# Layer 0 of a four-layer transformer kernel: order of the loads, place of the router's sums and of the mask's comparison

## The chip, the cores and the metric

The kernel runs on one core of one Trainium2 chip. The time is the device time of one execution in microseconds (us), as the median of three runs. Profiles come from one execution under the hardware profiler; times inside it count from the start of its span. TensorE (PE) does matrix products, VectorE (DVE) and ScalarE (ACT) work on rows of 128 partitions, GpSimd (POOL) sends the indirect DMAs here, and SyncE (SP) issues most of the plain DMAs, in its own order. PEld is TensorE's weight load.

## The reference, cut to what matters

Four layers, each of the form x = x + ffn(cond(x)), on x of shape (2, 1024, 256) in float32, so 2048 tokens. The change is in layer 0 and in one preparation for layer 1.

```python
def _L0_cond_ref(Efou, y, weight):
    ys = y * scale
    d = rsqrt(einsum('bi,io->bo', ys * ys, weight * weight) + EPS)
    return einsum('bsi,io->bso', Efou * ys[:, None, :], weight) * d[:, None, :]

def _L0_ffn_ref(x, gate_w, shared..., routed...):
    shared_out = _swiglu(x, shared_gate_w, shared_up_w, shared_down_w)   # width 512
    logits = x @ gate_w                                                  # 32 experts
    topk_ids, topk_val = argmax(logits), max(logits)
    xs = x * sigmoid(topk_val)
    # each token's row goes through the swiglu of its one expert (width 512)
    return shared_out + routed_out
```

Layer 1's attention takes a mask of (1024, 1024) bytes, `where(mask, scores, neg)`. The inputs have 1024 equal mask rows. The kernel compares them on the chip: where all rows are equal it uses a short form of layer 1, else a general one.

## The kernel before

x lies as `XT` (channels on partitions, two halves of 128 by 2048 tokens) and later as `Xt` (tokens on partitions). Layer 0, in `_layer0`, goes through these steps:

1. The conditioning weight `W` is loaded, squared (L425), and multiplied with the squared condition (`pd`, L429). Then eight products `ph` (L441) of 128x512 give `HT`, scaled by `dd` on ScalarE. `XT`'s first 1024 tokens are loaded by the kernel's entry function, the rest here (`_wload`, L84).
2. `_logits` gives 32 logits for each token; `_top` takes the maxima (L173) and their indices (L175).
3. `_route_static` counts, in one-hot rows `oh`, running sums `cum` and two products into `R` (L562, L564), which row of the DRAM buffer `xbuf` each token goes to: 96 rows for each of 32 experts, and 21 overflow tiles behind them. `xbuf` is filled with zeroes first by a DMA from `k.zero`, which is a piece of the same buffer `ACC` that holds the token rows `Hr` (row tile 15).
4. For 16 tiles of 128 tokens, `_token_major` (L350) turns `HT` into rows on TensorE, ScalarE scales them by the router's score, and GpSimd scatters them to `xbuf` (L281). The same is done for `XT` into `Xt` on VectorE (L461), without a scatter.
5. `shared(tb)` runs the shared expert for token block `tb` of 512 tokens: for each of 4 slices `f` of the width, products `spg` and `spu` (L1360), Silu (L1365), the product `sa` on VectorE (L1367), and four products into `spo` (L1370). Blocks 0 and 1 stand here, blocks 2 and 3 after the slots.
6. `_layer1_pre` loads layer 1's small weights, compares the mask's rows with row 0 (L667, L668, four pieces of 256 rows), sums the differences on TensorE (L672), and prepares layer 1's constants in small products.
7. 24 slots of 128 rows (`Split`): each loads its rows `xs` from `xbuf` (L297, only after all scatters), turns them (`ps_cm`, copied to `xsT`, L1523), and runs products `fpg`, `fpu` (L1659), the product `fa` on VectorE (L1694), turns `fpt`, copied to `faT` (L1670, L1671), and products `fpo` (L1677). Weights of the experts (three of 512 KB each) stream through a ring of 20 places of 512 KB (L400). Results go to `ybuf`.
8. The sum `rare` of "mask rows differ" and "overflow tiles used" decides by a branch whether overflow slots and the general layer 1 run. With these inputs neither runs.

The order of instructions on an engine comes from a scheduler that fills the engines by priority (program order) and by its own estimates of durations; semaphores are set from that order. `_behind(k, inst, ref)` orders one instruction after another for the scheduler without a wait; `_after` makes a wait. PSUM tiles with one `tag` share a number of buffers (`mm` 4, `t` 2, `o` 2). `hook` in `_shared` is called after each slice's products:

```python
        if hook:
            hook(f, mul, mm)
```

Of the kernel before, what the change touches and what calls it, by code (L numbers as in the profile page):

```python
# [8 lines left out]
F32 = mybir.dt.float32  # L9
# [255 lines left out]
class Rows:  # L265
# [30 lines left out]
    def load(self, dst, src):  # L296
        i = self.k.nc.sync.dma_start(dst, src)  # L297
        _after(self.k, i, self.new)
        self.read.append(i.ins.name)

# [45 lines left out]
def _token_major(k, psum, src, t):  # L346

    ps = psum.tile([P, 2, P], F32, name="ps_tm", tag="t", bufs=2)
    for c in range(2):
        k.nc.tensor.transpose(ps[:, c, :], src[:, c, t * P:(t + 1) * P], k.ident)  # L350
    return ps.rearrange("p c d -> p (c d)")
# [32 lines left out]
def _layer0(k):  # L384
# [11 lines left out]

    def weights(src):
        ws = [k.ring.take().rearrange("p (c f) -> p c f", f=f) for f in (F, F, D)]
        for w, n in zip(ws, ("L0_r1", "L0_r3", "L0_r2")):
            nc.sync.dma_start(w, A[n][src].rearrange("o (c p) f -> p (o c) f", p=P))  # L400
        return ws

    with ExitStack() as ctx:
# [4 lines left out]

        W, Wb0 = k.ring.take().rearrange("p (n c f) -> n p c f", n=2, c=2)
        W2, Wb1 = k.ring.take().rearrange("p (n c f) -> n p c f", n=2, c=2)  # L410
        _wload(nc, W, A["L0_cond_weight"])
        gw = rp.tile([P, 2, E], F32, name="l0_gw")
        _wload(nc, gw, A["L0_gate_w"])
        _wload(nc, XT[:, :, S:N], A["xT"][:, S:N])
# [4 lines left out]
        nc.vector.memset(k.Hr[:, :, D:], NONE)  # L419
        _zero_rows(k, ybuf[NS * T:(NS + NOV) * T, :])  # L420
# [28 lines left out]
        m8, ixf = _top(nc, rp, lg, E, "l0")  # L449
        score = rp.tile([P, NT], F32, name="l0_score")  # L450
        nc.scalar.activation(score, m8[:, :, 0], AF.Sigmoid)
        k.x.begin()
        rows, eid, nov, end = _route_static(k, rp, k.pre, psum, ixf, E, C, NOV, "l0")
        for t in range(NT):
            nc.scalar.activation(Ht[:, t, :], _token_major(k, psum, HT, t), AF.Copy,
                                 scale=score[:, t:t + 1])
            k.x.scatter(k.Hr[:, t, :], rows[:, t:t + 1])


        for t in range(NT):  # L460
            nc.vector.tensor_copy(Xt[:, t, :], _token_major(k, psum, XT, t))  # L461

        for tb in range(2):
            shared(tb)
        _layer1_pre(k, k.pre, psum)

        rare = k.pre.tile([1, 1], F32, name="l0_raref")
        nc.vector.tensor_tensor(rare, k.differf[0:1, :], end[0:1, E - 1:E], ALU.add)
        any_ = k.pre.tile([1, 1], I32, name="l0_rare")
        nc.vector.tensor_copy(any_, rare)  # L470
        _router_biases(k, psum)

        ws = {}
        slots = Slots(k, pool, psum)
        split = Split(k, pool, psum, slots, F)
        for i in range(NS):
            lo, cols = i * T, []
# [8 lines left out]
            split.slot(i, cols)  # L486
# [5 lines left out]
    k.yrows = (NS + NOV) * T  # L492
    free = k.ring.i, set(k.ring.held)

    def slots_over():
        k.ring.held = set(held)
# [47 lines left out]
    with cmp.Else():  # L544
        with tc_pool(k, "l0p", 2) as pool, tc_pool(k, "l0ps", 4, PSUM) as psum:
            one(rest())
# [3 lines left out]
def _route_static(k, pool, keep, psum, ixf, E, C, nov, name):  # L550
# [8 lines left out]
    for t in range(NT):  # L559
        nc.vector.tensor_add(cum[:, t + 1, :], cum[:, t, :], oh[:, t, :])  # L560
    R = psum.tile([P, NT, E], F32, name=name + "_R", tag="mm")
    nc.tensor.matmul(R.rearrange("p t e -> p (t e)"), k.before,  # L562
                     oh.rearrange("p t e -> p (t e)"), start=True, stop=False)
# [80 lines left out]

def _layer1_pre(k, pp, psum):
# [6 lines left out]
    with ExitStack() as ctx:  # L652
        pool = ctx.enter_context(tc_pool(k, "l1pr", 1))

        m0 = pool.tile([P, S], U8, name="l1_m0")
        nc.sync.dma_start(m0, A["mask"][0:1, :].to_broadcast([P, S]))

        k.mh = pp.tile([P, TB], U8, name="l1_mh")
        for g in range(4):
            q = slice(32 * g, 32 * g + 32)  # L660
            nc.gpsimd.tensor_copy(k.mh[q, :], m0[q, (g % 2) * TB:(g % 2 + 1) * TB])
        dif = pool.tile([P, 8], F32, name="l1_dif")
        for i in range(4):
            mm = pool.tile([P, 2, S], U8, name="l1_mm", bufs=2)
# [1706 lines left out]
```

## Time and profile before

| | us |
|---|---|
| median of 3 runs | 1553.33 (1551.42 to 1553.47) |
| profiled execution | 1554.72 |
| its span | 1553.0 |
| first product of TensorE | 9.81 |
| start of the logits' products | 28.2 |
| first turn of slot 0 | 107.03 |
| last product of the last slot, about | 269.9 |

The mean granted clock of TensorE over the span is 0.977 of full speed. HBM reads are 284.86 MB and writes 50.76 MB. A row of the timeline gives start, length, engine, source line, operation, result and operands, and in brackets how long the engine had been idle and what released it. A row of a table of stages gives busy time of each engine in a stretch of the span, the granted clock of TensorE (1.00 is full), and what the DMA engines moved. "SPq" is SP's queue of DMA issues.

### The profile page before, as it was taken

The page shows a single profiled execution, that of the slowest core. Times are in us where ns is not written, and L with a number is a line of the kernel's source. Part 1 is how long each engine was busy: PE and PEld are TensorE (multiplying, and loading weights), DVE is VectorE, ACT ScalarE, POOL GpSimd, SP SyncE. Part 2 cuts the span into 40 slices and gives each one's busy share as a digit, 9 for nine tenths or more (in the row PEclk, how much of TensorE's full clock was granted, in tenths as well). Part 3 has the DMA queues.
Part 4 walks back from the last instruction along what each step waited for, and adds up shares of the span by engine and source line. Part 5 has one row for each costly group of instructions (what it writes and reads, how often), then busy time and mean ns, then how long its engine had stood idle before and what let it go on. Part 6 is the DMA issues. An engine that isn't in the chain of part 4 may idle for free. (4 is left out here: it accounts for less than half of the span.)

```text
span 1553.0 us, 23694 instructions
## 1 busy us (share of the span) xinstructions
PE 1470.2 (95%) x8649; PEld 1021.0 (66%) x8652; DVE 478.2 (31%) x1596; ACT 303.9 (20%) x642; POOL 285.2 (18%) x317
## 2 busy tenths in 40 slices
PE   6989999999999999999999999999999989998897
PEld 2543333444555886555699999999985547864675
DVE  3732222324411444421111111111114414446432
ACT  2311212123111212211111111111111212126222
POOL 0400000300331441033001001010010253420342
PEclk9989999999999999999999999999999999999799
DMA  9859995923211684051053254155517437762470
GB/s 253 273 201 332 337 352 175 255 72 123 96 48 35 195 252 136 0 214 52 28 185 116 94 190 174 36 184 184 180 34 263 139 122 246 214 218 83 146 250 19
DMA packets 184239, 252.43 MB, mean 163 GB/s; under 512 B 17111, under 2 KB 137823, under 8 KB 184112
## 3 DMA queue, kind: packets, MB, share of 16 engines
q1 hardware_dynamic: 164448, 210.92, 42.2%
q0 software_dynamic: 14176, 36.63, 6.6%
q10 hardware_dynamic: 5488, 3.25, 0.7%
q8 instruction: 72, 1.18, 0.3%
q14 instruction: 55, 0.45, 0.1%
HBM read 284.86 MB, written 50.76 MB: 216 GB/s over the span
## 5 line engine op out<-in xcount | busy, mean ns | idle before, releaser
L1370 PE MATMUL spo<-ring,sa 128*128 128x256 f32 x768 | 192.5, 393 | 20.2 <-DVE sa L1367 15.1
L1370 PEld LDWEIGHTS spo<-ring,sa 128*128 128x128 f32 x768 | 140.7, 192 | 101.9 <-DVE sa L1367 71.5
L281 POOL DMA_INDIRECT tbuf<-ys,sdst x114 | 112.1, 984 | 509.4 <-ACT ys L1635 381.9
L1367 DVE TENSOR_TENSOR sa<-ssg,spu 128x512 f32<-128x512 f32 x96 | 65.8, 686 | 327.3 <-PE spu L1360 287.3
L1628 DVE TENSOR_TENSOR fa<-fsg,fpu 128x512 f32<-128x512 f32 x72 | 49.5, 687 | 316.0 <-PE fpu L1623 316.0
L1623 PE MATMUL fpu<-xsT,ring 128*128 128x128 f32 x1152 | 140.4, 275 | 0.0
L1623 PE MATMUL fpg<-xsT,ring 128*128 128x128 f32 x1152 | 140.3, 275 | 0.0
L1623 PEld LDWEIGHTS fpg<-xsT,ring 128*128 128x128 f32 x1152 | 137.1, 192 | 1.9
L1623 PEld LDWEIGHTS fpu<-xsT,ring 128*128 128x128 f32 x1152 | 134.4, 192 | 0.0
L1632 PE MATMUL fpo<-ring,fa 128*128 128x256 f32 x576 | 130.3, 379 | 0.0
L1365 ACT ACTIVATE ssg<-spg 128x512 f32<-128x512 f32 x96 | 57.3, 597 | 347.7 <-PE spg L1360 217.5
L1632 PEld LDWEIGHTS fpo<-ring,fa 128*128 128x128 f32 x576 | 106.7, 190 | 13.0
L1360 PE MATMUL spg<-HT,ring 128*128 128x512 f32 x192 | 102.1, 621 | 5.4 <-issue 2.8
L1360 PE MATMUL spg<-XT,ring 128*128 128x512 f32 x192 | 97.5, 599 | 0.1
L1360 PE MATMUL spu<-HT,ring 128*128 128x512 f32 x192 | 91.6, 596 | 0.0
L1360 PE MATMUL spu<-XT,ring 128*128 128x512 f32 x192 | 90.4, 592 | 0.0
L1599 PE MATMUL cph<-xsT,ring 128*128 128x128 f32 x624 | 83.9, 277 | 6.7 <-DMA ring<-in_L_r 3.7
L1599 PEld LDWEIGHTS cph<-xsT,ring 128*128 128x128 f32 x624 | 76.0, 192 | 10.4 <-DVE sn L1527 4.8
L1606 PE MATMUL cpo<-ring,ch 128*128 128x256 f32 x312 | 80.1, 380 | 0.8 <-ACT ch L1602 0.8
L1627 ACT ACTIVATE fsg<-fpg 128x512 f32<-128x512 f32 x72 | 43.0, 597 | 169.7 <-PE fpg L1623 169.7
L1360 PEld LDWEIGHTS spu<-XT,ring 128*128 128x128 f32 x192 | 36.6, 191 | 43.8 <-issue 43.6
L1360 PEld LDWEIGHTS spu<-HT,ring 128*128 128x128 f32 x192 | 36.6, 194 | 41.9 <-issue 41.7
(574 smaller groups left out, 1656.5 us busy)
## 6 DMA issues: line engine op xcount, KB each, us to landing
ring<-in_L_w SPq DMA_DIRECT2D x108, 1024.0 KB
ring<-in_L_r SPq DMA_DIRECT2D x96, 512.0 KB
ring<-in_L_r SPq DMA_DIRECT2D x156, 256.0 KB
xs<-xbuf SPq DMA_DIRECT2D x138, 129.0 KB
ring<-in_L_W SPq DMA_DIRECT2D x32, 512.0 KB
yt<-tbuf SPq DMA_DIRECT2D x48, 256.0 KB
xbuf<-ACC SPq DMA_DIRECT2D x1, 6063.0 KB
ring<-in_L_s SPq DMA_DIRECT2D x6, 512.0 KB
```

Of the source, the lines that this page charges most:

```text
L281: i = k.nc.gpsimd.indirect_dma_start(out=self.ap, out_offset=bass.IndirectOffsetOnAxis(ap=idx, axis=0), in_=rows, in_offset=None, **end)
L1360: mm = nc.tensor.matmul(ps, W[:, c, f * P:(f + 1) * P], X[:, c, cols], start=c == 0, stop=c == 1)
L1365: k.silu = nc.scalar.activation(sg, pg, AF.Silu)
L1367: mul = nc.vector.tensor_mul(a, sg, pu)
L1370: mm = nc.tensor.matmul(po[g // 2][:, g % 2, :], a[:, g * P:(g + 1) * P], W2[:, f, :], start=f == 0 and g % 2 == 0, stop=f == nf - 1, skip ...
L1599: made = [nc.tensor.matmul(ph[:, f, :], R1[:, c, f * P:(f + 1) * P], xT[:, c, :], start=c == 0, stop=c == 1) for f in range(2) for c in ra ...
L1606: made = [nc.tensor.matmul(po, h[:, f, :], R2[:, f, :], start=f == 0, stop=f == 1) for f in range(2)]
L1623: made = [nc.tensor.matmul(ps[:, j, :], W[:, c, (f0 + j) * P:(f0 + j + 1) * P], xT[:, c, :], start=c == 0, stop=c == 1) for ps, W in ((pg, ...
L1627: nc.scalar.activation(sg, pg, AF.Silu)
L1628: nc.vector.tensor_mul(a[:, f0:f0 + 4, :], sg, pu)
L1632: made = [nc.tensor.matmul(po, a[:, f, :], W2[:, f, :], start=f == 0, stop=f == 4 * nh - 1) for f in range(4 * nh)]
```

## The change

- **Loads.** The conditioning weight is issued before `XT`; `XT` comes in four blocks of 512 tokens, then `gate_w`, then the shared weights. Four products of a tile of ones stand at the start of TensorE's work (`warm0`).
- **Clearing.** The filler column of `Hr` is set for tiles 0 to 14 only; tile 15 has it from `k.zero`. The 21 overflow tiles of `ybuf` are cleared in `slots_over`, in the branch for overflow.
- **Router.** Indices, `_route_static`, the turns of `HT` and the scatters move into the hook of shared block 0: all of the routing and tiles 0 to 7 at `f = 0`, tiles 8 to 15 at `f = 1`, `XT`'s turns for tiles 0 to 7 at `f = 2, 3`, and for tiles 8 to 15 in block 1. `_behind` ties index instructions to `mul` and TensorE's to `mm` of that slice.
- **Weights of experts 0 to 4** are issued before the slots' row loads, which are ordered behind the last of these 15 loads.
- **Mask.** The comparison leaves `_layer1_pre` for `_mask_rows`, a generator that is advanced once before each odd slot up to 17; it works in eight pieces of 128 rows. `rare` is formed after the slots' loop.

```diff
+        warm = psum.tile([P, 4, P], F32, name="warm0", tag="mm")
+        for _ in range(4):
+            nc.tensor.matmul(warm, k.ones, _bc(k.ones, 1, [P, 4, P]), start=True, stop=True)
...
         _wload(nc, W, A["L0_cond_weight"])
         gw = rp.tile([P, 2, E], F32, name="l0_gw")
+        for tb in range(NB):
+            _wload(nc, XT[:, :, tb * TB:(tb + 1) * TB], A["xT"][:, tb * TB:(tb + 1) * TB])
         _wload(nc, gw, A["L0_gate_w"])
-        _wload(nc, XT[:, :, S:N], A["xT"][:, S:N])
...
-        nc.vector.memset(k.Hr[:, :, D:], NONE)
-        _zero_rows(k, ybuf[NS * T:(NS + NOV) * T, :])
+        nc.vector.memset(k.Hr[:, 0:NT - 1, D:], NONE)
...
-        k.x.begin()
-        rows, eid, nov, end = _route_static(k, rp, k.pre, psum, ixf, E, C, NOV, "l0")
-        for t in range(NT):
-            nc.scalar.activation(Ht[:, t, :], _token_major(k, psum, HT, t), AF.Copy,
-                                 scale=score[:, t:t + 1])
-            k.x.scatter(k.Hr[:, t, :], rows[:, t:t + 1])
-        for t in range(NT):
-            nc.vector.tensor_copy(Xt[:, t, :], _token_major(k, psum, XT, t))
-        for tb in range(2):
-            shared(tb)
+        def stream(t, mm):
+            nc.vector.tensor_copy(Xt[:, t, :], _token_major(k, psum, XT, t, mm))
+
+        def lead(f, mul, mm):
+            if f == 0:
+                ix = rp.tile([P, NT, 8], U32, name="l0_ix", tag="ix")
+                for t in range(NT):
+                    _behind(k, nc.vector.max_index(ix[:, t, :], m8[:, t, :], lg[:, t, :]), mul)
+                ixf = rp.tile([P, NT, 8], F32, name="l0_ixf", tag="ixf")
+                nc.vector.tensor_copy(ixf, ix)
+                k.x.begin()
+                got[:] = _route_static(k, rp, k.pre, psum, ixf, E, C, NOV, "l0", mm)
+            if f < 2:
+                for t in range(8 * f, 8 * f + 8):
+                    nc.scalar.activation(Ht[:, t, :], _token_major(k, psum, HT, t, mm), AF.Copy,
+                                         scale=score[:, t:t + 1])
+                    k.x.scatter(k.Hr[:, t, :], got[0][:, t:t + 1])
+            else:
+                for t in range(4 * f - 8, 4 * f - 4):
+                    stream(t, mm)
+
+        got = []
+        shared(0, lead)
+        rows, eid, nov, end = got
+        shared(1, lambda f, mul, mm: [stream(t, mm) for t in range(8 + 2 * f, 10 + 2 * f)] if f < 4 else None)
         _layer1_pre(k, k.pre, psum)
...
-        ws = {}
-        slots = Slots(k, pool, psum)
+        ws = {e: weights(slice(e, e + 1)) for e in range(5)}
+        slots = Slots(k, pool, psum, ref=sent[-1])
         split = Split(k, pool, psum, slots, F)
+        muls = []
+        mask = _mask_rows(k, k.pre, pool, psum, muls)
         for i in range(NS):
+            if i < 18 and i % 2 == 1:
+                next(mask)
...
-            split.slot(i, cols)
+            muls.append(split.slot(i, cols))
...
     def slots_over():
+        k.yrows = (NS + NOV) * T
+        nc.vector.memset(k.zero[:, 0:D], 0.0)
+        _zero_rows(k, ybuf[NS * T:(NS + NOV) * T, :])
...
-def _route_static(k, pool, keep, psum, ixf, E, C, nov, name):
+def _route_static(k, pool, keep, psum, ixf, E, C, nov, name, ref):
...
+    i = nc.tensor.matmul(R.rearrange("p t e -> p (t e)"), k.before,
+                         oh.rearrange("p t e -> p (t e)"), start=True, stop=False)
+    _behind(k, i, ref)
...
+def _mask_rows(k, pp, pool, psum, muls):
+    nc, A = k.nc, k.A
+    m0 = pool.tile([P, S], U8, name="l1_m0", bufs=1)
+    nc.sync.dma_start(m0, A["mask"][0:1, :].to_broadcast([P, S]))
...
+    for i in range(8):
+        mm = pool.tile([P, S], U8, name="l1_mm", bufs=2)
+        nc.sync.dma_start(mm, A["mask"][i * P:(i + 1) * P])
+        yield
+        ne = pool.tile([P, S], U8, name="l1_ne", bufs=1)
+        _behind(k, nc.vector.tensor_tensor(ne, mm, m0, ALU.not_equal), muls[-1])
+        nc.vector.tensor_reduce(dif[:, i:i + 1], ne, AX.X, ALU.add)
+    d1 = pool.tile([P, 1], F32, name="l1_d1", bufs=1)
+    nc.vector.tensor_reduce(d1, dif, AX.X, ALU.add)
+    pd = psum.tile([P, 1], F32, name="l1_pd", tag="t", bufs=2)
+    nc.tensor.matmul(pd, k.ones, d1, start=True, stop=True)
...
+            load = self.k.x.load(self.xs[i], self.k.xbuf[i * P:(i + 1) * P, :])
+            if self.ref is not None:
+                _behind(self.k, load, self.ref)
...
-    _wload(nc, k.XT[:, :, 0:S], A["xT"][:, 0:S])
```

## The prediction

> **What bounds the kernel now.** I read the page's totals first, then a table of stages over the first 114 us, then the timeline of single waits, because the change touches nothing behind layer 0's 24 expert slots. The page says TensorE is busy 95% of the span, so only time in which it idles, or runs at a lowered clock, can be won.
>
> ```profile
> span 1553.0 us, 23694 instructions
> PE 1470.2 (95%) x8649; PEld 1021.0 (66%) x8652; DVE 478.2 (31%) x1596; ACT 303.9 (20%) x642; POOL 285.2 (18%) x317
> ```
>
> The chain that ended last gives nothing for the first 140 us, so the stages have to speak (columns: window, length, busy time and instructions of PE, PEld, DVE, ACT, POOL, granted clock, DMA share, GB/s):
>
> ```profile
> 0.00:10.00 10.00, 0.19 (x1) 0.19 (x2) 1.64 (x11) 1.28 (x1) 2.04 (x15) 1.00 0.64 212
> 9.80:28.20 18.40, 18.39 (x40) 8.79 (x40) 2.85 (x18) 5.01 (x8) 0.00 (x0) 1.00 1.11 287
> 28.20:48.00 19.80, 12.05 (x48) 6.01 (x48) 12.84 (x80) 6.34 (x13) 0.00 (x0) 0.74 1.10 288
> 48.00:82.00 34.00, 34.00 (x134) 20.42 (x132) 26.81 (x41) 10.66 (x18) 22.00 (x20) 1.00 0.68 231
> 82.00:107.03 25.03, 19.61 (x102) 12.99 (x101) 9.44 (x19) 4.08 (x8) 0.00 (x0) 0.84 0.73 251
> ```
>
> TensorE idles 9.8 us at the start, 7.7 us in 28.2 to 48 (routing) and 5.4 us in 82 to 107, and the clock falls to 0.74 and 0.84 there. In the timeline (start, length, engine, line, operation, in brackets the idle time before and its releaser) one sees by what:
>
> ```profile
> 9.81 1.87 PE L429 MATMUL pd<-l_ys,ring 128*128 128x2 f32 x8 [9.81 <-DVE ring L425]
> ...
> 42.95 0.09 DVE L419 MEMSET ACC<- 128x32 f32 x1 [2.29 <-DMA xbuf<-ACC]
> ...
> 43.15 1.13 PE L564 MATMUL l_R<-l_cum,ones 128*128 128x512 f32 x2 [2.00 <-DVE l_cum L560]
> ...
> 79.67 0.34 SPq L297 DMA_DIRECT2D xs<-xbuf  x1
> ...
> 83.56 2.29 DVE L667 TENSOR_TENSOR l_ne<-l_mm,l_m 128x2048 uint8<-128x2048 uint8 x1 [4.45 <-DMA l_mm<-in_mask]
> ...
> 86.50 3.78 PE L1370 MATMUL spo<-ring,sa 128*128 128x256 f32 x8 [4.03 <-DVE sa L1367]
> ```
>
> VectorE waits for the zeroing of xbuf at L419, and R behind it. SP's queue stands from 63 us until the scatters are done (79.67). Behind that stands the last mask load; VectorE waits for it, and shared block 1's product `sa` behind VectorE.
>
> From 107 us on the slots run without holes. A slot takes 6.18 us, or 6.97 us where two row tiles are turned first (121.15 to 127.33 to 134.30), and TensorE hardly waits for a weight.
>
> **Start.** Before, TensorE's first product waits for the weight, queued behind 1 MB of XT. It then runs cold: fp32 instructions of 512 columns come every 0.86 us until 17.2 us, then every 0.43. The change puts the weight (0.25 MB) ahead of XT and splits XT. The 2 KB `cT` load, issued at 0.83, was used at 4.44; so I put the weight at 5 to 6 us and XT's first quarter at 7 to 8 (estimates from that and the 1.3 MB landed by 9.06). The four added products of ones are 8 instructions x 0.86 = 6.9 us, from 1.2 (`ones` is set at 0.92) to 8.1. So they, not the loads, set the start: pd 8.1 to 9.05, then 32 instructions x 0.43 = 13.8, end 22.9 against 28.2: **-5.3**.
>
> Here the Trainium skill ("TensorE: Matmul & The Clock Gate", Part 1) gives a warm-up of about 3.4 us of sustained activity. By it the last four added instructions would take 0.43 each and the stage end 1.7 us earlier (-7.0). The trace needed 7.4 us here and 5.7 us after the hole at 86.5. I take the trace.
>
> Against splitting speaks the Trainium skill's "DMA: Bandwidth & Descriptors", Bandwidth: transfers of at least 1 MiB for 75% of peak; XT goes from two of 1 MB to four of 0.5 MB. Its 6.15 us for 1 MB (78%), had every half to be paid alone, would put XT's fourth quarter at some 15 to 18 us (estimate); TensorE wants it at 9.05 + 10.3 = 19.4, so the sum stays. The slots' own loads are 0.5 MB and move 350 GB/s, so I keep 10 to 12 us.
>
> **Logits to slot 0.** Before, 28.2 to 107.03 = 78.8 us. The work in it at full clock: spg and spu 64 x 0.43 = 27.5; spo 64 x 0.215 = 13.8; ps_tm 64 x 0.108 = 6.9; logits, their turn, R and cnt 4.0; layer 1's preparation 5.1; the mask's sum 0.3. Together 57.6, so 21.2 are lost: 13.2 idle, 8 clock and gaps.
>
> The change puts max_index and all of the routing behind the first `sa` product, with shared block 0 beside it, and ties the 32 turns of rows to its steps. The scheduler orders TensorE by its own estimates, which I can't see. Before, R's halves stood 2.4 and 2.0 us waiting. I take 3 us of such stalls (0 where shared products stand between, 10 where both halves are placed as badly as before and the clock falls too).
>
> The hole at 82.5 (4.0) and its cold stretch to 92.2 (half of 5.7, 2.9) go with the mask's comparison. So does the wait at L419, since the memset leaves row 15 alone. Layer 1's preparation stays serial: 1.5 idle, and 3 for clock and gaps. Thus 57.3 + 3 + 1.5 + 3 = 64.8, slot 0 at 22.9 + 64.8 = 87.7 against 107.0; this part gives **-14.0**.
>
> Can rows and weights be there? Logits end like before 3.4 us ahead of `lg`: 26.3, maxima 28.6, Sigmoid and Silu tables (1.28 each) and `sa` about 31.5. The old chain from index to rows took 33.84 to 53.02, less 2.3 for the wait: 16.9, and 2 for three `sa` between: rows at 50.4. Sixteen scatters took 53.9 to 78.0; four lasted 2.2 to 2.4 us, mostly under a mask comparison, instead of 0.96, so without it about 19 to 20: 70. xs is issued at about 72 and landed near 75.5, 12 us before slot 0. The xbuf zeroing landed at 42.95 with 2.7 MB of ybuf zeroes behind it; without them no later, and before 50. That removal therefore gives **0**; without this cover the scatters, then slot 0, would move one for one.
>
> The 15 loads of experts 0 to 4 now pass ahead of xs on SP: about 15 x 0.55 = 8 us of issue and 7.9 MB, 23 us at 350 GB/s, behind the zeroing; done by about 65, while xs waits until 72 anyhow: **0**. On SP the mask's nine loads leave the front and stand among the slots' weights. Each needs a buffer that VectorE freed two pieces before, so I price that at 0; if one waits, all weights behind it wait.
>
> **Slots.** Eight comparisons and eight reductions of 128x1024 bytes come to VectorE, half of the 2.28 us of the old 128x2048 rows: 1.14 each, 2.28 a slot. The gap that they fall into, from this timeline (`faT` of the same stretch starts at 129.88):
>
> ```profile
> 120.67 0.76 DVE L1523 COPY xsT<-ps_cm 128x256 f32<-128x256 f32 x2 [1.44 <-PE ps_cm L359]
> 125.67 0.69 DVE L1694 TENSOR_TENSOR fa<-fsg,fpu 128x512 f32<-128x512 f32 x1 [1.54 <-PE fpu L1659]
> 131.84 0.69 DVE L1694 TENSOR_TENSOR fa<-fsg,fpu 128x512 f32<-128x512 f32 x1 [1.54 <-PE fpu L1659]
> 133.82 0.75 DVE L1523 COPY xsT<-ps_cm 128x256 f32<-128x256 f32 x2 [1.30 <-PE ps_cm L359]
> ```
>
> After an even slot's `fa` VectorE is free for 3.5 us, after an odd slot's only 1.3 us before `xsT`, which TensorE awaits. The pieces are tied to even `fa`: they fit, price 0. On the other parity each would hold `xsT` by 1.0, 8 in all. I take **+1**, near the fitting end, because up to slot 16 the pairs stand before even slots. The mask's sum (0.3 on TensorE) and the branch's flag lie well before the last slot: 0, or up to 1.5 if the flag is ordered last. The added `ref`s only order; the ybuf clearing sits in a branch not taken here.
>
> **Sum.** -5.3 - 14.0 + 1 = -18.3. The profiled execution took 1554.7 us (span 1553.0): 1536.4. The median of the runs is 1.4 lower: **1535**.
>
> **Rivals.** (1) Routing only half hidden: both halves of R stall TensorE for some 4 us each, with cold clock after, as the old order did. That takes 8 to 10 off: about 1544. For it: the old trace shows TensorE standing there though shared products were ready. Against: the order is now tied to the shared block. (2) The scatters set slot 0. They must be 12 us later than reckoned, rows at 62; if at 66, slot 0 is 4 us later, and the time 1539; far worse only with the zeroing held up by weights, at rows near 72: 1545. (3) Slower: the slots starve. After slot 0 about 81 weight loads (42.5 MB), 2.7 of xs, 3.1 of ybuf and 1.2 of mask must pass in the 148 us up to slot 23's first product: 335 GB/s, where 323 over the stretch and 350 in its middle were seen, at TensorE's demand. If mask loads stop SP's queue so that the mean falls to 49.5/167 = 296 GB/s the gain is gone; at 280 the slots take 29 us more, and the result is about 1564. Against: the five experts held ahead are 25 us of cover. (4) It does nothing: the scheduler, moved by the new orders, builds the old holes elsewhere: 1553.
>
> **Chances.** Forecast 0.60 (its own range 1529 to 1540), (1) 0.15, (2) 0.08, (3) 0.12, (4) 0.05. A measurement tells 0.2%, 3 us, from no change. Faster 0.60 + 0.15 + 0.08 = 0.83, less a sliver of bad cases of (1) and (2), 0.82; same 0.05; slower 0.13. The range goes from the forecast's low end with the skill's clock and no stall, 1528, to 1550, beyond which lie (3), (4) and that sliver.
>
> **What would show it.** Right: pd near 8 us and instructions 0.43 apart soon after; no idle on R beyond 3 us; no hole at a `sa` in shared block 1; ps_cm of slot 0 near 88; slots still 6.2 and 7.0 us; the comparisons directly behind even `fa`. Wrong: PE waiting for `l_cum` or `l_oh`, for xs at slot 0, or for ring loads within the slots; `xsT` starting later behind a comparison.

## The result and the profile after

The changed kernel took 1559.33 us (median of 20 runs, 1553.04 to 1566.73), the kernel before 1553.80 in the 20 runs measured beside it. The ratio is 1.0037, with a 95% interval of 1.0024 to 1.0051: slower by 0.4%, where 1535 and "faster" had been forecast. In two other groups of runs, told of below, the same kernel came out 0.2% faster than the kernel before, and 0.5% slower.

The profiled execution took 1560.12 us, its span 1558.4. First the totals of the page of the changed kernel:

```profile
span 1558.4 us, 23706 instructions
PE 1473.9 (95%) x8660; PEld 1020.1 (65%) x8660; DVE 479.7 (31%) x1604; ACT 305.2 (20%) x643; POOL 281.2 (18%) x317
```

The span grew by 5.4 us: TensorE's busy time by 3.7, in which the 5.87 us of the added products of ones are counted, and its idle time by 1.7. So the idle time that was to go did not go. The table of stages of the changed kernel (window, length, busy time and instructions of PE, PEld, DVE, ACT, POOL, granted clock, DMA share, GB/s) says where; its windows are the start, `ph`, routing, two stretches of the shared blocks, and the slots:

```profile
0.00:7.72 7.72, 5.87 (x8) 2.23 (x9) 1.49 (x11) 1.28 (x1) 2.04 (x15) 1.00 0.47 123
7.72:22.54 14.82, 14.82 (x40) 6.89 (x40) 2.69 (x18) 5.01 (x8) 0.00 (x0) 1.00 1.10 317
22.54:47.40 24.86, 21.61 (x87) 11.17 (x86) 15.15 (x82) 11.08 (x17) 0.00 (x0) 1.00 1.11 232
47.40:74.14 26.74, 13.84 (x54) 8.67 (x53) 7.17 (x20) 6.17 (x12) 15.52 (x16) 0.80 1.06 378
74.14:105.22 31.08, 28.62 (x140) 17.51 (x140) 9.22 (x23) 5.29 (x10) 2.42 (x4) 0.94 0.22 67
105.22:278.70 173.48, 160.49 (x1432) 61.86 (x1427) 59.22 (x109) 33.48 (x73) 0.00 (x0) 0.97 0.81 278
```

The logits start at 22.54 instead of 28.2. Routing had 12.05 us of TensorE's work in 19.8 us before, and now has 21.61 in 24.86. But from 47.4 to 74.1 TensorE works for only 13.84 of 26.74 us, at a clock of 0.80. Slot 0 starts at 105.22, 1.8 us earlier than before and not 19. The slots take 173.5 us; the same stretch before took 165.57, from 107.03 to 272.6. The rest of the kernel is as long as before.

The timeline of the changed kernel (start, length, engine, line, operation, in brackets the idle time before and its releaser) shows the start and what stands in that stretch:

```profile
1.14 5.87 PE L416 MATMUL warm<-ones 128*128 128x512 f32 x8 [1.14 <-DVE ones L92]
...
6.97 0.69 DVE L436 TENSOR_TENSOR ring<-ring 128x512 f32<-128x512 f32 x1 [2.38 <-DMA ring<-in_L_cond_weight]
...
7.72 1.05 PE L440 MATMUL pd<-l_ys,ring 128*128 128x2 f32 x8 [0.71 <-DVE ring L436]
...
14.76 20.41 SPq L84 DMA_DIRECT2D l_wq<-in_L_Wq  x1
...
40.26 1.89 SPq L84 DMA_DIRECT2D l_sim<-in_L_sim  x1
42.20 2.28 SPq L759 DMA_DIRECT2D l_gts<-in_L_gates  x1
...
49.70 0.19 DVE L762 TENSOR_TENSOR l_sq<-l_sim 128x32 f32<-128x32 f32 x1 [6.31 <-DMA l_sim<-in_L_sim]
49.89 0.21 ACT L760 ACTIVATE l_gts<-l_gts 128x16 f32<-128x16 f32 x1 [7.79 <-DMA l_gts<-in_L_gates]
...
52.44 1.11 PE L351 MATMUL ps_tm<-ident,HT 128*128 128x128 f32 x4 [5.01 <-ACT ACC L481]
...
66.66 0.69 DVE L398 TENSOR_TENSOR Xt<-spo,Xt 128x512 f32<-128x512 f32 x1 [3.75 <-PE spg L1404]
71.56 0.69 DVE L398 TENSOR_TENSOR Xt<-spo,Xt 128x512 f32<-128x512 f32 x1 [4.21 <-remote]
...
73.66 0.42 DVE L467 COPY Xt<-ps_tm 128x256 f32<-128x256 f32 x1 [1.41 <-issue]
74.14 0.69 PE L351 MATMUL ps_tm<-ident,XT 128*128 128x128 f32 x2 [7.88 <-issue]
...
105.22 1.12 PE L362 MATMUL ps_cm<-ident,xs 128*128 128x128 f32 x4
```

There are two holes. **The first** (47.4 to 52.4): VectorE stands 6.3 us in the middle of the routing's chain for `l_sim`, ScalarE 7.8 us for `l_gts`, two loads of a few KB for layer 1. SP issued them at 40 and 42 us, because its queue had stood at `l_wq` from 14.76 to 35.2, behind the 6 MB zeroing of `xbuf`. **The second** (66.3 to 74.1): TensorE's row names no cause, but it starts when VectorE's copy of `ps_tm` at 73.66 has freed a place in PSUM (in e11 below the row names VectorE). VectorE's two sums come 3.8 and 4.2 us after the instruction before them. TensorE's last product of the `spo` that they read had ended at 64.95.

The kernel before had the same late loads, and they cost nothing there. From its timeline:

```profile
13.31 20.46 SPq L343 DMA_DIRECT2D ybuf<-ACC  x1
33.82 10.07 SPq L84 DMA_DIRECT2D l_wq<-in_L_Wq  x1
...
51.57 0.37 SPq L84 DMA_DIRECT2D l_sim<-in_L_sim  x1
```

SP's queue stood 30 us in all behind the two clearings, and `l_sim` went out at 51.57 us; but `l_sq` stood far behind in VectorE's order: it ran at 88.56 us, and did not wait.

In the slots there are three places. The waits of SP's queue in the changed kernel (us in all, times, longest):

```profile
SPq L696 <- DVE l_ne L699: 17.4, 6, 5.6
```

Six mask loads stood 17.4 us for the comparison that frees their buffer, with row loads behind them. The timeline of the changed kernel's TensorE, with idle time only:

```profile
208.05 0.41 PE L362 MATMUL ps_cm<-ident,xs 128*128 128x128 f32 x2 [1.64 <-DMA xs<-xbuf]
222.24 0.38 PE L704 MATMUL l_pd<-l_d,ones 128*128 128x1 f32 x2 [1.58 <-DVE l_d L702]
223.46 1.45 PE L1705 MATMUL fpg<-ring,xsT 128*32 128x512 f32 x8 [0.55 <-DVE l_rare L518]
```

TensorE waits for rows, at slot 17 for the mask's reduction, and one product later for the flag.

### The profile page after: what moved, and what is told of

Read it like the earlier page. It is cut to its first block, busy times and chain, and to the rows that moved or that the text cites. A ratio compares the mean times of both kernels' runs of the same rounds, so it can differ in the third digit from the quotient of the medians.

```text
span 1558.4 us, 23706 instructions
## 1 busy us (share of the span) xinstructions
PE 1473.9 (95%) x8660; PEld 1020.1 (65%) x8660; DVE 479.7 (31%) x1604; ACT 305.2 (20%) x643; POOL 281.2 (18%) x317
## 5 line engine op out<-in xcount | busy, mean ns | idle before, releaser
L1409 ACT ACTIVATE ssg<-spg 128x512 f32<-128x512 f32 x96 | 57.3, 597 | 347.5 <-PE spg L1404 250.5
```

Source lines behind the costliest of these rows:

```text
L1409: k.silu = nc.scalar.activation(sg, pg, AF.Silu)
```

## Experiments

Each group of runs was made together, with the kernel before measured in the same group; only ratios within a group are compared closely. "Slot 0" is the start of its first turn, "slots" the time from the first `fpg` of slot 0 to that of slot 23, both from one profiled execution of each kernel; before: 107.03 and 152.4, changed: 105.22 and 159.2. The kernel before has a profile of the first measurement only, so where a slot 0 or a stretch of slots is set against it, two groups are compared.

| Run | Group, before (us) | median (us) | ratio to before, 95% | slot 0 | slots |
|---|---|---|---|---|---|
| e1 small loads first | A, 1545.29 | 1536.91 | 0.9949 (0.9935 to 0.9963) | 89.46 | 160.1 |
| e2 four mask buffers | A | 1535.93 | 0.9940 (0.9924 to 0.9957) | 97.01 | 157.5 |
| e3 lazy weights | A | 1545.20 | 0.9996 (0.9981 to 1.0011) | 97.22 | 159.5 |
| e4 before + start | A | 1534.82 | 0.9932 (0.9912 to 0.9952) | 99.17 | 151.3 |
| e5 changed again | B, 1548.69 | 1546.33 | 0.9983 (0.9969 to 0.9996) | 97.55 | 159.4 |
| e6 before + mask | B | 1550.63 | 1.0013 (0.9998 to 1.0029) | 103.33 | 161.1 |
| e7 sum late | B | 1541.77 | 0.9954 (0.9938 to 0.9970) | 97.29 | 159.5 |
| e8 repaired | B | 1528.79 | 0.9865 (0.9838 to 0.9892) | 88.97 | 151.0 |
| e9 mask loads by GpSimd | C, 1553.81 | 1561.39 | 1.0045 (1.0030 to 1.0060) | 110.56 | 154.5 |
| e10 repaired, sum early | C | 1551.24 | 0.9982 (0.9965 to 1.0000) | 98.22 | 155.4 |
| e11 changed again | C | 1560.32 | 1.0052 (1.0035 to 1.0070) | 104.73 | 158.3 |
| e12 repaired + ybuf clear | C | 1545.76 | 0.9948 (0.9929 to 0.9966) | 98.64 | 151.9 |
| e13 repaired again | D, 1543.54 | 1530.37 | 0.9909 (0.9877 to 0.9941) | 88.84 | 151.4 |
| e14 repaired, lazy | D | 1528.29 | 0.9884 (0.9841 to 0.9927) | 90.67 | 152.1 |
| e15 no scatters | D | 1563.30 (one run) | | 92.21 | 152.1 |
| e16 memsets ahead | D | 1527.14 (one run) | | 89.09 | 152.2 |
| e17 loads last | E, 1543.17 | 1528.52 | 0.9906 (0.9890 to 0.9923) | 92.23 | 152.0 |
| e18 no scatters | E | 1551.60 (one run) | | 89.18 | 150.6 |

### The first hole: two small loads (e1)

```diff
+        k.sim = k.pre.tile([P, 2, 16], F32, name="l1_sim")
+        _wload(nc, k.sim, A["L1_sim"])
+        k.gts = k.pre.tile([P, 16], F32, name="l1_gts")
+        nc.sync.dma_start(k.gts, A["L1_gates"].to_broadcast([P, 16]))
         k.x = Rows(k, xbuf, [_zero_rows(k, xbuf)])
...
-        _wload(nc, sim, A["L1_sim"])
-        nc.sync.dma_start(k.gts, A["L1_gates"].to_broadcast([P, E]))
```

(The last two lines are in `_layer1_pre`; the added ones stand on L428.)

> The changed kernel, with only the two small loads l_sim and l_gts issued ahead of xbuf's zeroing. Theory 'small loads': the hole of 47.4 to 52.4 us on TensorE is VectorE and ScalarE standing for these two loads (6.31 and 7.79 us). Then rows come at about 46 us instead of 52, the hole goes with its cold stretch, slot 0 starts about 7 us earlier (near 98) and the time is about 1552. Rival 'order': the hole comes from the order of the turns and the routing's chain itself; then TensorE still stands some 4 us before the turn of HT, slot 0 stays near 105, and the time near 1559. The second hole (66.3 to 74.1) shows here too unless it was a single event of the profiled execution.

Timeline of e1, the same instructions:

```profile
14.69 0.34 SPq L428 DMA_DIRECT2D l_gts<-in_L_gates  x1
15.15 0.62 SPq L344 DMA_DIRECT2D xbuf<-ACC  x1
15.82 20.07 SPq L84 DMA_DIRECT2D l_wq<-in_L_Wq  x1
17.86 0.19 DVE L762 TENSOR_TENSOR l_sq<-l_sim 128x32 f32<-128x32 f32 x1 [7.37 <-DMA l_sim<-in_L_sim]
19.42 0.22 ACT L760 ACTIVATE l_gts<-l_gts 128x16 f32<-128x16 f32 x1
```

The queue still stands 20 us behind the zeroing; the two loads are now ahead of it, and `l_sq` and `l_gts` are done at 18 and 20 us, in time that nobody needs. The first hole is gone, TensorE works without a gap from 37 to 79 us, and slot 0 starts at 89.46. In e2 and e3 of the same group, the changed kernel with other mask buffers and with later expert loads, which have the first hole and not the second, it starts at 97.01 and 97.22, up to 7.8 us later. From 47.4 to 74.14 TensorE idles 5.8 us in e3, at a clock of 0.87, and not at all in e1, at 1.00. The theory of the small loads holds, and the rival "order" falls. By the medians e1 is 8.3 us faster than e3. (The expectation's 98 still counted with the second hole, which this group does not show.) The slots are no better than in the changed kernel.

### The second hole (e3, e5, e11, and e13 to e18)

```diff
-        ws = {e: weights(slice(e, e + 1)) for e in range(5)}
-        slots = Slots(k, pool, psum, ref=sent[-1])
+        ws = {}
+        slots = Slots(k, pool, psum)
```

> The changed kernel, without the early issue of the 15 expert loads: they are issued slot by slot as in the kernel before. TensorE, VectorE and ScalarE keep their orders. Theory 'crowding': the hole of 66.3 to 74.1 us comes from the DMA engines being full with the 15 loads (378 to 393 GB/s from 50 to 74 us), which makes VectorE's instructions late. Then the hole is gone, slot 0 starts 8 to 10 us earlier (near 96), and the time is about 1550, or 1555 if the first slots wait for weights. Rival 'scatters': the hole comes from GpSimd's scatters at the same time; then it stays, slot 0 near 105, time near 1559. Rival 'once': the hole is absent here and in the other runs as well.

e3 has no second hole, but e1 and e2 of the same group, with all 15 loads, have none either. So the group could not decide, and e5 ran the changed kernel unaltered:

> The changed kernel itself, unaltered, on the chip of the other experiments. With the four-buffer mask its first 97 us had the same orders and no hole at 66 to 74 us. Theory 'single event': the hole belongs to the one profiled execution or to its chip; then slot 0 starts near 97 here, the slots take some 8 us more than before, and the ratio to the kernel before is about 0.996 (97 + 8 against 107). Rival 'the change makes it': the hole of 7 to 8 us comes again, slot 0 near 105, ratio 1.002 to 1.005, and a second buffer pair for the mask would have to be what removed it.

Table of stages of e5, the stretch that held both holes and the next one:

```profile
47.40:74.14 26.74, 20.32 (x78) 12.70 (x78) 9.71 (x26) 6.83 (x14) 14.93 (x16) 0.87 1.07 380
74.14:97.55 23.41, 20.94 (x117) 13.29 (x115) 6.61 (x17) 4.64 (x9) 3.05 (x5) 0.96 0.34 110
```

Only the first hole is in it, and slot 0 starts at 97.55; the kernel is 0.17% faster than before. It would have been easy to take the second hole for one bad execution. But e11, the same kernel in group C, has it again:

> The changed kernel once more, unaltered. If the hole of 66 to 74 us is a single event, it is absent again, slot 0 is near 97.5 us and the ratio near 0.998. If it is back, slot 0 is near 105 and the ratio 1.002 to 1.005.

Timeline of e11:

```profile
65.84 0.69 DVE L398 TENSOR_TENSOR Xt<-spo,Xt 128x512 f32<-128x512 f32 x1 [2.82 <-PE ps_tm L351]
70.05 0.69 DVE L398 TENSOR_TENSOR Xt<-spo,Xt 128x512 f32<-128x512 f32 x1 [3.52 <-remote]
...
71.13 0.69 PE L351 MATMUL ps_tm<-ident,XT 128*128 128x128 f32 x2 [4.76 <-DVE Xt L398]
```

All four kernels of group C show it, also e10 and e12, where everything comes some 6 us earlier: there the hole lies at 59 to 65 us. The late VectorE instructions are the two sums of `spo` into `Xt` at L398 (in e12 only the second of them) and the copies behind them. None of the other groups shows it, with the same orders and the same DMA rate (e5 380 GB/s, the changed kernel 378). It goes with the kernel before, too, which took 1554 us in the first measurement and in group C, and 1543 to 1549 in the others.

Three things on record narrow it. It is not the chip alone: groups C and D ran on the same one, some 16 minutes apart, and only C shows the hole. It is not this stretch alone: from the first product behind the slots to the end of the span, where the change touches nothing, the traces of the first measurement and of group C take 1277.5 to 1286.8 us, and those of the other groups, e15 and e18 apart, 1269.7 to 1276.4. And the traces themselves differ: those of the first measurement and of group C hold some 14000 semaphore events, all others 17400 to 17600. A wait can therefore have lost its releaser in the rows with the hole ("remote", "issue"), so they cannot tell what VectorE waited for; whether the recording itself has a part in the hole was not tested.

Three causes were put to the test, in groups D and E, on the repaired kernel described below: fewer loads beside the scatters (e14, the diff of e3; e17, also with the diff of e3, every expert load behind the first row load), no scatters (e15 and e18, which leave out the move of the token rows), and another place of the instructions in VectorE's stream (e16, with 24 memsets ahead). The edits of e17, of e15 and e18, and of e16:

```diff
-            sent.append(nc.sync.dma_start(w, A[n][src].rearrange("o (c p) f -> p (o c) f", p=P)))
+            sent.append(nc.sync.dma_start(w, A[n][src].rearrange("o (c p) f -> p (o c) f", p=P)))
+            [_behind(k, sent[-1], r) for r in first]
...
+        slots.fetch(0); first.append(slots.first)
```

```diff
-                    k.x.scatter(k.Hr[:, t, :], got[0][:, t:t + 1])
```

```diff
+        pad = rp.tile([P, 1], F32, name="pad"); [nc.vector.memset(pad, 0.0) for _ in range(24)]
         ys = rp.tile([P, 2, 2], F32, name="l0_ys")
```

> The repaired kernel once more, as the control of this group. On the chip where the changed kernel shows no hole at 60 to 74 us it took 0.9865 of the kernel before. If the chip of this group makes VectorE's instructions late while the scatters and the 15 expert loads run, as in the first profile of the changed kernel, TensorE stands 4 to 8 us between 56 and 70 us, slot 0 starts at 96 to 99 us and the ratio is about 0.993 to 0.996. If not, slot 0 is at 89 us and the ratio at 0.987.

> The repaired kernel without the early issue of the 15 expert loads (six are issued ahead of the first row load, the others slot by slot); the orders of TensorE, VectorE and ScalarE are the same. Theory 'crowding': with fewer loads beside the scatters VectorE is on time, slot 0 is at 89 us and the time at or under that of the control, by 7 us or more where the control shows the hole. Rivals 'scatters' and 'place in the program': the hole is as in the control.

> The repaired kernel without the 16 scatters, so xbuf stays zero and the routed experts work on zero rows: it leaves out the move of the token rows. Theory 'scatters': GpSimd's scatters, which issue every 1.27 us in the stretch, keep VectorE waiting; without them VectorE is on time and slot 0 at 89 us or earlier even where the control shows the hole. Theory 'crowding': the 15 loads alone keep the DMA engines full to about 70 us, and the hole stays where the control has it.

> The repaired kernel with 24 small memsets of a scratch column put ahead of VectorE's work, some 12 of them before the routing as the order shows (they take under 0.1 us each in idle time). Theory 'place in the program': the late instructions of VectorE (two sums of spo into Xt, then copies of ps_tm) are late because of where they stand in VectorE's stream of instructions[...]; moved by the memsets, others are late, and these are on time. Theories 'crowding' and 'scatters': the same instructions are late as in the control, or none if the control shows none.

> The repaired kernel with all expert loads behind the first row load on SP, so that none runs beside the scatters; the orders of TensorE, VectorE and ScalarE are the same. If the chip of this run is one where the hole shows (the kernel before near 1554 us): theory 'crowding' expects VectorE on time between 56 and 70 us and slot 0 near 90 us, the theories 'scatters' and 'place in the program' a hole of 4 to 8 us and slot 0 at 96 to 99 us. Where the kernel before is near 1545 us no hole is expected by any of them; then slot 0 and the first slots show what the early issue is worth: 90 us and the control's time within 3 us if nothing, 95 us or more if the first weights come late.

> The repaired kernel without the 16 scatters (xbuf stays zero, the move of the token rows is left out, and later layers route other data), once more. Where the kernel before is near 1554 us: 'scatters' expects VectorE on time and slot 0 near 90 us, 'crowding' the hole of 4 to 8 us. Where it is near 1545 us, no hole by any theory, and only the first 92 us can be compared.

The control e13 shows no hole, and neither do the others, so none of these six could tell the causes apart. One form of the third cause can be looked up in the traces: that VectorE's instructions are fetched late. In the changed kernel, e9 and e11 no packet of an instruction queue moved from 42 to 80 us, so what ran late had been fetched before. **The cause of the second hole stays open.** (e15 and e18 leave the expert rows at zero and take longer behind layer 0, with 24257 and 24254 instructions where e13 has 23698; only their first 92 us are compared.)

What they do show: the 15 early loads are worth nothing that can be measured. e14 differs from its control by less than the intervals, and e17, in a group of its own, has the control's ratio (0.9906 and 0.9909). Slot 0 at 92.23 in e17 looks like a loss of 3.4 us, but the turn of its logits is 2.7 us later than in e13 already (27.73 and 25.07).

### The start alone (e4)

The kernel before, with these lines of the change and nothing else:

```diff
+        for _ in range(4):
+            nc.tensor.matmul(warm, k.ones, _bc(k.ones, 1, [P, 4, P]), start=True, stop=True)
...
         _wload(nc, W, A["L0_cond_weight"])
+        for tb in range(NB):
+            _wload(nc, XT[:, :, tb * TB:(tb + 1) * TB], A["xT"][:, tb * TB:(tb + 1) * TB])
         _wload(nc, gw, A["L0_gate_w"])
-        _wload(nc, XT[:, :, S:N], A["xT"][:, S:N])
...
-    _wload(nc, k.XT[:, :, 0:S], A["xT"][:, 0:S])
```

> The kernel before, with only the start of the change: four products of ones, the conditioning weight loaded first, XT in four blocks. Theory 'start carries': the logits' products start near 22.5 us instead of 28.2 and 5 us of it reach the end: 1549. Rival 'eaten': routing waits for the zeroing of xbuf (landed at 42.95 us) and the mask's load, neither of which comes earlier, so slot 0 stays near 107 and the time within 2 us of 1554.

It carries through: 10.5 us under the kernel before (0.9932), more than the start itself and than the theory's 5. Logits begin at 23.56, 4.6 earlier, slot 0 is 7.9 earlier, and its slots take 1.1 us less, against the profile of before. Between logits and slot 0, the 2.0 us that TensorE waited for R's second half (L564) are gone; the rest is not traced further. By the ratios this small part alone does better than the whole change.

### The mask in the slots (e2, e6, e7, e9, e10)

e6 is the kernel before with only the mask moved: `_mask_rows` and its steps in the slots' loop as in the change, the comparison out of `_layer1_pre`, the flag behind the loop.

```diff
+        mask = _mask_rows(k, k.pre, pool, psum, muls)
         for i in range(NS):
+            if i < 18 and i % 2 == 1:
+                next(mask)
...
-            split.slot(i, cols)
+            muls.append(split.slot(i, cols))
```

> The kernel before, with only the mask's comparison moved into the slots and the flag formed after their loop. Theory 'exchange': ahead of the slots the wait at sa (4.0 us) and its cold stretch (2.9) go, in the slots 6 to 8 us come (waits for xs behind mask loads 3, the sum at slots 17 and 18 some 3 to 5): the time within 2 us of the kernel before. Rival 'free comparisons', as forecast: the slots gain 1 us only and 6 us are won.

The exchange it is: the ratio is 1.0013; slot 0 comes 3.7 us earlier and the slots take 8.7 us longer, against the profile of before. Three runs take the loss apart. In e2 the mask loads have four buffers, in e9 GpSimd issues them instead of SP:

```diff
-        mm = pool.tile([P, S], U8, name="l1_mm", bufs=2)
+        mm = pool.tile([P, S], U8, name="l1_mm", bufs=4)
```

```diff
-        nc.sync.dma_start(mm, A["mask"][i * P:(i + 1) * P])
+        nc.gpsimd.dma_start(mm, A["mask"][i * P:(i + 1) * P])
```

> The changed kernel, with four buffers for the mask's pieces instead of two, so that a mask load waits for a comparison six slots back and not two. Theory 'queue': the slots' loss of 6.8 us against the kernel before comes from SP's queue standing at mask loads; then no mask load stands, the waits for xs fall from 3.0 to about 1.2 us in sum, and 4 us or more of the 6.8 come back: about 1555. Rival 'mask sum': the loss sits at slots 17 and 18, where TensorE waits for the mask's sum and VectorE for the flag; then 4 to 5 us stay and the time is 1557 to 1558. The first 105 us have the same orders as the changed kernel, so this also shows whether the hole of 66 to 74 us comes again.

> The changed kernel, with the eight mask loads issued by GpSimd, which is idle in the slots, instead of by SP. Bytes, buffers and comparisons stay. Theory 'queue': SP stands at its mask loads (six waits, 17.2 us in sum) and issues row and weight loads late; without that the slots go back to about 151 to 153 us from the first fpg to the last, less 2 to 3 us for the sum at slots 17 and 18, and the ratio to the kernel before falls to about 0.994. Rival 'bytes': the 1.2 MB in a stretch where the DMA engines move 330 to 360 GB/s are what delays the rows; then the slots stay above 157 us and the ratio near 0.998.

Waits of e2, SP's queue and TensorE (us in all, times, longest):

```profile
SPq L696 <- DVE xsT L1569: 0.4, 1, 0.4
...
PE ps_cm L362 <- DMA ring<-in_L_r: 1.5, 1, 1.5
PE ps_cm L362 <- DMA xs<-xbuf: 1.1, 3, 0.4
```

SP hardly stands at mask loads any more, and the waits for rows fall from 4.0 us in e5 to 1.1, but one of 1.5 for weights is new; 2.0 us of slots come back against e3 of its group (1.9 against e5), where the theory "queue" wanted 4. The medians say more: e2 is 9.3 us faster than e3, which differs from it in the early loads too. Its profiled execution is the slowest of its twelve, 6 us above the median, so the size that it shows is not firm.

e9 has the same bytes in the same stretch. TensorE's waits for rows in e9, and below them those in e11 of its group:

```profile
PE ps_cm L362 <- DMA xs<-xbuf: 0.7, 1, 0.7
...
PE ps_cm L362 <- DMA xs<-xbuf: 3.8, 3, 1.9
```

The slots take 154.5 us in e9 and 158.3 in e11: 3.8 us back. So it was SP's queue and not the bytes. e9 is no faster than e11 all the same: in its profile slot 0 is 5.8 us later, with a longer second hole (8.41 us) and the start and `l_sim` 1 to 2 us later. Whether the new issuer has a part in that is not shown.

The sum: e7 moves it four slots later, e10 moves it back in the repaired kernel.

```diff
-            if i < 18 and i % 2 == 1:
+            if i < 18 and i % 2 == 1 or i == 21:
                 next(mask)
...
     nc.vector.tensor_reduce(d1, dif, AX.X, ALU.add)
+    yield
```

> The changed kernel, with the mask's last product and its copies four slots later (before slot 21 in the program), the reduction left where it was. Theory 'sum': TensorE no longer waits 1.6 us for the reduction nor 0.55 for the flag, the clock stays full, slots 17 and 18 take 6.0 to 7.1 us each and some 3 to 4 us of the slots' loss come back; with slot 0 where the changed kernel has it. Rival 'queue': the waits for xs at slots 12 and 15 make most of the loss, and less than 2 us come back.

> The repaired kernel with the mask's sum where the changed kernel has it (slot 17). If the sum itself costs what the changed kernel showed there (1.6 us and 0.55 us of waits and a stretch of cold clock), the slots take 2 to 4 us more than the repaired kernel's 151.0, and the ratio is about 0.988 to 0.989. If TensorE only waits there because row loads were late, the slots stay at 151 to 152 us.

e7 is 4.6 us faster than e5 by the medians. Its profiled execution, 1548.58 us and the slowest of its runs, doesn't show it: the rows of slot 15 came 2.95 us late there. e10 shows it cleanly, in its timeline of TensorE from 204 us on:

```profile
204.67 1.94 PE L1705 MATMUL fpg<-ring,xsT 128*64 128x512 f32 x8 [0.52 <-DVE xsT L1569]
212.51 0.38 PE L704 MATMUL l_pd<-l_d,ones 128*128 128x1 f32 x2 [1.58 <-DVE l_d L702]
...
213.72 3.51 PE L1705 MATMUL fpg<-ring,xsT 128*32 128x512 f32 x16
...
221.49 1.92 PE L1705 MATMUL fpg<-ring,xsT 128*32 128x512 f32 x16
```

The same two slots in e12, the repaired kernel of the same group:

```profile
204.94 1.94 PE L1705 MATMUL fpg<-ring,xsT 128*64 128x512 f32 x8 [0.30 <-DVE xsT L1569]
...
211.01 1.90 PE L1705 MATMUL fpg<-ring,xsT 128*32 128x512 f32 x16
...
218.31 1.92 PE L1705 MATMUL fpg<-ring,xsT 128*32 128x512 f32 x16
```

With no row late, TensorE still waits 1.58 us at `l_pd`, and the `fpg` behind it takes 3.51 us instead of 1.92. The two slots take 9.1 and 7.8 us, in e12 6.1 and 7.3. The sum in its old place costs 3.5 us. (e12 also clears `ybuf`, which bears on the time ahead of the slots.)

### All repairs together (e8, e12)

e8 joins e1, e7 and one more edit: the mask comes in one load of 1 MB into `ACC`, free once the scatters have read it, so no mask load stands among the slots' weights.

```diff
+    mms = k.acc[:, 0:2 * S].bitcast(U8).rearrange("p (t s) -> p t s", t=8)
+    nc.sync.dma_start(mms, A["mask"].rearrange("(t p) s -> p t s", p=P))
     for i in range(8):
-        mm = pool.tile([P, S], U8, name="l1_mm", bufs=2)
-        nc.sync.dma_start(mm, A["mask"][i * P:(i + 1) * P])
+        mm = mms[:, i, :]
         yield
```

> The changed kernel with three repairs: the two small loads ahead of the zeroing, the whole mask loaded at once into ACC behind the scatters (one load of 1 MB ahead of slot 1, none within the slots), the mask's sum four slots later. If the losses are those three, slot 0 stays near 89.5 us, the slots go back to about 152 us from the first fpg to the last as before, and the time is 7 to 8 us under the kernel with the small loads alone: a ratio near 0.990 to the kernel before. Rival 'comparison in the slots costs by itself': the slots stay above 156 us, and the ratio near 0.995.

Table of stages of e8, from 47.4 us on:

```profile
47.40:74.14 26.74, 26.74 (x102) 15.70 (x101) 9.37 (x19) 4.18 (x9) 15.57 (x16) 1.00 1.06 385
74.14:88.97 14.83, 12.37 (x89) 8.98 (x88) 4.47 (x13) 3.51 (x7) 2.43 (x4) 0.92 0.65 220
88.97:253.80 164.83, 157.35 (x1433) 61.44 (x1426) 58.65 (x108) 33.51 (x73) 0.00 (x0) 0.99 0.85 288
```

The stretch of the holes is full at full clock, slot 0 starts at 88.97, and the slots take 151.0 us with all eight comparisons in them. e8 is 19.9 us faster than the kernel before in its group, and 17.5 faster than the changed kernel there. In group D (e13) the gain is 13.2 us; the intervals, 0.9838 to 0.9892 and 0.9877 to 0.9941, just meet. So it beats the kernel before in both groups, and the changed kernel in the one where that ran; in group C, with the second hole, e12 (nearly the same kernel) still wins 0.5% over the kernel before.

e12 puts the clearing of `ybuf` back:

> The repaired kernel with the clearing of ybuf's 2.75 MB put back behind xbuf's zeroing. Theory 'covered', as forecast: scatters begin no later than TensorE needs, slot 0 stays within 1 us of 89 and the time within 2 us of the repaired kernel. Rival: the clearing ends some 7 to 8 us after xbuf's, holds back the 15 expert loads and with them the row loads; then the weights or rows of slot 0 come late and slot 0 moves by 3 us or more.

Slot 0 at 98.64 is that of e10 beside it (98.22), which has no clearing; both carry the second hole. In e12 the 15 expert loads begin 6 us later (48.45 and 42.33), but the first row load goes out at 72.10, in e10 at 72.58. So the clearing delays nothing that slot 0 waits for, and no cost of it is seen. Whether slot 0 would stay at 89 without the hole was not run.

## Why the prediction was wrong

- **Start, -5.3: right in size, in part by luck.** Logits start 5.7 us earlier. What set the start was another: the step said the products of ones set the start; they were done at 7.0, and the weight, which landed only then, did (VectorE's square at 6.97, TensorE 0.71 us idle before `pd` at 7.72). So the products ran 1 us shorter and the weight came 1 to 2 us later than reckoned. The eight instructions took 5.87 us in the profile above; the row taken gave 6.9, and the Trainium skill's 3.4 us of warm-up ("TensorE: Matmul & The Clock Gate", Part 1) gives 5.2 (an estimate: four at 0.86 us, four at 0.43). Neither is firm: over the 18 profiles with these products they took 5.22 to 6.64 us, 12 of them nearer to 5.2 and 6 nearer to 6.9. Splitting `XT` cost nothing: `ph` and `pd` kept TensorE busy for all of their 14.82 us.
- **Logits to slot 0, -14.0: failed.** It was +3.9 (82.7 us against 78.8) in the first profile, and -3.8 in e5. The stall of R was no more than taken (1.2 us, 3 taken), and the sum of the work holds: in e8 TensorE is busy 60.9 us of this part, where 57.3 and 3 for clock and gaps were forecast. The step that failed is "Layer 1's preparation stays serial": it was costed as a block between the shared blocks and slot 0, but its two instructions that wait for a load, `l_sq` and `l_gts`, moved into the routing on VectorE and ScalarE, ahead of their data. The step looked at the instructions of the diff, and not at those beside it that the scheduler would move. SP's queue was in view (the zeroing landed at 42.95), and the loads of layer 1 behind it were not followed. The wait costs 7.8 us (e1 against e3). With the two loads ahead of the zeroing (e8) the step measures -12.2 (66.6 us), the first scatter goes out at 48.92 and the last at 68.11 (rows at 50.4 and the last at 70 were forecast), and slot 0 starts at 88.97, where 87.7 was forecast. (The trace of before has three scatters of 2.2 to 2.4 us, not four; the estimate of 19 to 20 us for all of them came out at 20.2.)
- **The second hole** has no term in the sum, and its cause is open. Where it shows, slot 0 is 7 us later (e11 against e5), and the sign goes with it: 0.5% slower with it, 0.2% faster without. With the first hole and the -12.2 of e8 it makes +2.8 of the +3.9.
- **The 15 loads, 0, and the clearing of ybuf, 0: right as far as was seen** (e14 and e17; e12, under the second hole).
- **Slots, +1: failed, by its "0" for the mask loads and its "0, or up to 1.5" for the sum.** The comparisons themselves fit behind even `fa` at 1.22 us each (1.14 reckoned), and cost nothing (e8: 151.0 us with them, 152.4 before without). But "each needs a buffer that VectorE freed two pieces before" took the loads' place in the program for the time they are issued: SP issued the third piece at 125.93 us, as soon as the first comparison had freed its buffer, and VectorE took it up at 151.00, four slots later. With SP that far ahead, six loads stood 17.4 us, and the rows behind them came late: 3.8 us (e9). The mask's sum stalls TensorE, since its product stands in order ahead of `ps_cm` and behind a reduction that had only just begun: 3.5 us (e10). Together, 7.3 us, they account for what the slots lost: 6.9 us in the changed kernel, 5.9 to 7.7 in its repeats and e1.
- **Rivals.** Ahead of the slots the nearest is (4), given 0.05: the scheduler builds the holes elsewhere, 1553 us. The first hole is of that kind, and e5 came out 2.4 us under its kernel before; but (4) named no instruction. In the slots it is (3), the slots starve because mask loads stop SP's queue. Its mechanism came, its size did not: 3.8 us and not 29. Rival (1) looked for the loss at R; it was at two loads of layer 1.

So the forecast's sum of -18.3 was near that of a kernel that could be built: against the profile of before, e8's slot 0 gives -18.1 and the stretch from there to the end of the slots -0.7. By the medians the repaired kernel won 19.9 us in one group and 13.2 in the other.

## What to carry to other kernels

When work is moved, follow the neighbours too: an instruction of another part that waits for a load can slide into the chain that was just made short, and its load may be late behind a long transfer in its queue (20 us here). A load with a recycled buffer, in a queue that runs ahead, waited here for the consumer of the old data and held all behind it; give it its own space or its own queue. A product whose input is just being made goes where TensorE passes long after, not at the next place in program order.

## What was not expected of the hardware

SP's queue stood some 20 us at the transfer issued right after the zeroing of `xbuf` (6 MB): 20.41 us at `l_wq` in the changed kernel, 20.07 in e1. With the clearing of `ybuf` behind the zeroing (e12) it stood 19.02 us at that instead, and then 10.46 us more at `l_wq`. The profile of before already shows it (20.46 and 10.07 us), so it could have been reckoned with.

The same program with the same orders ran with and without the second hole in different groups of runs, 7 us apart at slot 0 and 0.7% apart in its ratio to the kernel before (0.9983 and 1.0052). A single profile of the changed kernel would have had either reading.
